# Layer 0 mixing on one core: product tiles with channels outermost, and the second gate spread over two passes

## The chip, the cores and the metric

The kernel runs on one core of a Trainium2 chip. The metric is the device time of one execution in microseconds, as the median of several runs.

## The reference, cut to what matters

The program is a chain of four image layers over x of shape (8, 56, 56, 192) in float32. Only layer 0 is touched. For every image it projects the normalised input three times (p, q and v, each with 576 channels and a silu), multiplies q by v, and convolves the product along the rows and along the columns with a decaying Toeplitz kernel of its own per channel. Then the sum of both is gated by p and projected back:

```python
qv = q * v
o1 = _toeplitz(qv.reshape(b * h, w, D1), a1).reshape(b, h, w, D1)
o2 = _toeplitz(jnp.transpose(qv, (0, 2, 1, 3)).reshape(b * w, h, D1), a2)
o2 = jnp.transpose(o2.reshape(b, w, h, D1), (0, 2, 1, 3))
out = p * (o1 + o2)
return out @ o_w.T + o_b
```

The result is added to the image, whose statistics the next layer uses.

## The kernel before, in words

Layer 0 has two steps. Step one computes q times v for all images and writes the operands of the convolution to two tensors in device memory, `left` and `right`. Step two, `layer0_mix`, is where the change lies.

**Products.** For one channel, both convolutions together are one matrix product: 56 x 128 by 128 x 56, where half of the 128 rows hold the Toeplitz matrix and half hold qv. The 576 channels are nine blocks of 64. A block is loaded by two transfers of 1.8 MB, `lt` and `rt`, from SyncE's queue (`layer0_block`); there are two buffers of each. From a block, eight channels (or twice eight) at a time are copied into a packed left operand `lc` by GpSimd and a packed right operand `rc`, alternately by VectorE and ScalarE (`layer0_operand`, L460). Each has three buffers, so copies run three iterations ahead of the products. `layer0_products` (L468) multiplies them into one of two PSUM tiles `op`, and ScalarE copies the result into a tile `o` in SBUF (L664 and L667).

**Passes.** The 576 channels of an image are worked off in three passes (`PASSES`). Passes one and two each take four blocks, two channels at once (on partitions 0 to 55 and 64 to 119), in 16 iterations; pass three takes the last block, one channel at once, in 8 iterations. Every pass allocates a tile `o` of 120 partitions from a pool of two buffers, laid out row of the image first, channel last: `o[partition, h, channel]`. The copy turns each result into this order by a strided view of PSUM.

**Gates.** When a pass is complete, its gate runs in steps, one or two of them after the products of each iteration of the following pass. The generators `layer0_gate` (for passes one and two) and `layer0_gate_last` (for pass three) yield between steps. For each of four tiles of 392 positions (times two halves), `layer0_gate` projects x to p for two groups of 128 channels (L478, PSUM tile `pj`), applies the silu on ScalarE into `pp` (L485), transposes the matching part of `o` on TensorE by seven transposes a half (L490, PSUM tile `ot`), multiplies `pp` by it on VectorE (L495), and multiplies by the output weights in three parts (L501, PSUM tile `y`), which VectorE adds to the image x (L507 and L509). The projection of the next tile is put ahead, between the transposes of the present one. `pj`, `ot` and `pp` have one buffer each. `layer0_gate_last` does the same for 64 channels, two tiles at a time, with narrower transposes (L552) in 8 steps in all.

A transpose loads its part of `o` as the stationary operand (128 channels of one image row for each partition) and streams an identity matrix through it.

**Order.** In `layer0_mix` the program order is written out by hand for TensorE, ScalarE, VectorE and GpSimd: each engine executes in the order in which the code issues. An iteration is: the products, the copy of the result into `o`, the copies for the operand three iterations ahead (the last operand of a block also issues the transfers of the block after next), then gate steps, then a step of side work. Side work is the normalised image `xn` for the gates (`normed`, L597, ScalarE, from iteration 10 of pass one; one buffer) and the statistics of the finished image (L607). The number of gate steps per iteration is, before the change:

```python
for _ in range((at // 8 % 2, 1, 2)[p]):
    next(gate, None)
```

So the last gate of the previous image takes a step in every other iteration of pass one, gate one takes one step in every iteration of pass two, and gate two takes two steps in every iteration of pass three. What is left of a gate is run at the end of its pass. After the last image the block buffers are closed (`loaded`), which lets the transfers for layer 1 into their place start; then the last gate of the last image runs alone, with the store and the statistics.

Of the kernel before, what the change touches and what calls it, by code (L numbers as in the profile page):

```python
# [24 lines left out]
NSUB = D1 // 64  # L25
# [66 lines left out]
def kernel(ctx: ExitStack, tc: tile.TileContext, a: dict, out: bass.AP):  # L92
# [377 lines left out]
    def layer0_gate(g, o, x, xn, pool, psum, w_p, w_o):  # L470
# [16 lines left out]
        def turn(t, s, pp):  # L487
            ot = psum.tile([128, 8, 128], F32, name="ot", bufs=1)
            for i in range(7):
                nc.tensor.transpose(  # L490
                    ot[:, i, 0:64 + W], o[:, H // 2 * s + 7 * t + i], ident[0:64 + W, 0:64 + W]
                )
# [19 lines left out]
        pp = new()  # L512
        silu(0, project(0, 0), pp)
        yield
        for t in range(NTH):
            silu(1, project(t, 1), pp)
            turn(t, 0, pp)
            yield
            if t + 1 < NTH:
                ps = project(t + 1, 0)  # L520
            turn(t, 1, pp)
            yield
            out(t, 0, pp)
            out(t, 1, pp)
            yield
            out(t, 2, pp)
            if t + 1 < NTH:
                pp = new()
                silu(0, ps, pp)
            yield  # L530

    def layer0_gate_last(o, x, xn, pool, psum, w_p, w_o):
# [4 lines left out]
        for t in range(0, NTH, 2):  # L537
# [12 lines left out]
            for s in range(2):  # L550
                for i in range(7):
                    nc.tensor.transpose(  # L552
                        ot[:, s, i * W:(i + 1) * W], o[0:W, 14 * s + 7 * (t // 2) + i, :], ident[0:W, 0:W]
                    )
# [25 lines left out]
    def layer0_mix(pool, raws, psum, ops, w_p, w_o, loaded):  # L580
# [44 lines left out]
        def right_operand():  # L625
            i = len(rcs)
            if i < len(todo):
                b, s, d0, nu = todo[i]
                rcs.append(layer0_operand(copies[i % 2], blocks[b * NSUB + s][1], "rc", 3, d0, nu, pool))

        def left_operand():
            i = len(lcs)
            if i < len(todo):
                b, s, d0, nu = todo[i]
                k = b * NSUB + s
                lcs.append(layer0_operand(nc.gpsimd.tensor_copy, blocks[k][0], "lc", 3, d0, nu, pool))
                if i + 1 < len(todo) and todo[i + 1][1] != s:
                    block(k + 2)
# [3 lines left out]
        for _ in range(3):  # L642
            right_operand()
            left_operand()
        n, gate, side, xn, before = 0, iter(()), iter(()), None, None
        for b in range(nimg):
            for p, (chunks, subs) in enumerate(PASSES):
                nu = len(chunks)
                o = pool.tile([64 + W, H, 128], F32, name="o")
                if p == 0 and b:  # L650
                    gate = layer0_gate_last(before, x[b - 1], xn, pool, psum, w_p, w_o)
                elif p:
                    gate = layer0_gate(p - 1, before, x[b], xn, pool, psum, w_p, w_o)
# [6 lines left out]
                for at in range(0, 64 // nu * len(subs), 8):  # L660
                    layer0_products(ops[n % 2], nu, lcs[n], rcs[n])
                    part = 64 * (nu - 1) + W
                    if p < 2:
                        nc.scalar.copy(o[0:part, :, at:at + 8], ops[n % 2][0:part].rearrange("p d h -> p h d"))  # L664
                    else:
                        two = o[0:part, 0:H // 2].rearrange("p (q i) (u d) -> p q u i d", i=7, u=2)
                        nc.scalar.copy(  # L667
                            two[:, :, :, :, at:at + 8],
                            ops[n % 2][0:part].rearrange("p d (q u i) -> p q u i d", u=2, i=7),
# [1091 lines left out]
```

## Time and profile before

| what | value |
|---|---|
| median of 3 runs | 5717.95 us (5717.43 to 5723.02) |
| profiled execution | 5735.38 us |
| its span | 5733.6 us |
| mean granted TensorE clock | 0.956 |
| TensorE busy | 5143.6 us, 90% of the span |
| products L468, 9216 matmuls | 354.7 us busy, first 788.9 us, last 2015.6 us |
| transposes L490, 896 | 119.9 us busy, 274 ns mean |
| transposes L552, 224 | 17.2 us busy, 225 ns mean |
| operand copies L460 by GpSimd, 320 | 587.2 us busy, 1853 ns mean |

Busy times of matmuls include the latency of each, and matmuls overlap; what one costs in a row of equals is read from the distance between starts. A float32 matmul of the program stands as two in the trace, a transpose as one. A line that begins with two numbers in the timeline gives start and length in microseconds, and in brackets how long the engine had been idle and which instruction ended that. A window's line gives its length, the busy time of each engine with its number of instructions, the granted clock, the share of the DMA engines' time and the rate in GB/s.

### The profile page before, as it was taken

Reading aid. Unit: us, or ns where it says so; the run is one execution under the profiler, and the core shown is the slowest. Engines: PE = TensorE matmul, PEld = TensorE weight load, DVE = VectorE, ACT = ScalarE, POOL = GpSimd, SP = SyncE. Lnnn points to the kernel's source line nnn. Section 1 sums busy time; section 2 is a strip of 40 time slices with the busy share of each in tenths; the row PEclk is TensorE's granted clock in tenths of the full one; section 3 lists DMA queues with packets and bytes.
Section 4 is the critical chain, followed back from the end, with each engine's and each line's share of the span. In section 5 each row is a group of like instructions: output and inputs, shape, how many; then the busy total and the mean of one; then the engine's idle time right before and its main releaser. Section 6 shows DMA issues by size and latency. Waiting matters only on the chain. (4 is left out here: it accounts for less than half of the span.)

```text
span 5733.6 us, 113240 instructions
## 1 busy us (share of the span) xinstructions
PE 5143.6 (90%) x49446; PEld 3417.5 (60%) x49446; DVE 3084.6 (54%) x4087; ACT 2285.5 (40%) x3100; POOL 1839.6 (32%) x1583
## 2 busy tenths in 40 slices
PE   7899968898999869999997989999798798999999
PEld 6798855565566535555554757776344597444444
DVE  4555534545445445666664868888778212433331
ACT  3344444444444423333332015454476300433333
POOL 5555554444444424333442013333011101101100
PEclk9999979999999989999998989999899898999999
DMA  6888895666666532222223856775677687212211
GB/s 155 226 228 225 219 307 224 246 251 240 249 234 254 209 94 70 78 74 74 78 66 91 266 229 216 232 242 188 173 226 209 228 328 289 73 62 77 79 39 26
DMA packets 556148, 1013.75 MB, mean 177 GB/s; under 512 B 256104, under 2 KB 479684, under 8 KB 528884
## 3 DMA queue, kind: packets, MB, share of 16 engines
q1 hardware_dynamic: 542896, 956.63, 52.2%
q0 software_dynamic: 8512, 40.62, 2.2%
q10 hardware_dynamic: 4244, 9.26, 0.6%
q8 instruction: 389, 6.37, 0.5%
q14 instruction: 107, 0.88, 0.0%
HBM read 676.92 MB, written 345.97 MB: 178 GB/s over the span
## 5 line engine op out<-in xcount | busy, mean ns | idle before, releaser
L460 POOL COPY lc<-lt 128x896 f32<-128x896 f32 (+1 forms) x320 | 587.2, 1853 | 640.9 <-PE op L468 600.3
L427 PE MATMUL qv<-w_qv_sb,x 64*112 64x256 f32 (+1 forms) x5376 | 686.9, 409 | 14.9 <-DVE act L433 11.0
L427 PEld LDWEIGHTS qv<-w_qv_sb,x 64*112 64x112 f32 x5376 | 605.9, 175 | 85.1 <-DVE act L433 21.1
L433 DVE TENSOR_TENSOR act<-qv,b_qv 112x640 f32<-112x640 f32 x448 | 318.5, 752 | 322.7 <-PE qv L427 233.2
L437 ACT ACTIVATE act<-act 112x640 f32<-112x640 f32 x448 | 300.5, 684 | 415.6 <-DVE act L433 405.1
L403 POOL TENSOR_TENSOR qv<-act 112x320 f32<-112x320 f32 x448 | 346.3, 797 | 291.2 <-ACT act L437 212.5
L468 PE MATMUL op<-rc,lc 128*56 128x56 f32 x9216 | 354.7, 224 | 77.4 <-POOL lc L460 29.9
L468 PEld LDWEIGHTS op<-rc,lc 128*56 128x56 f32 x9216 | 330.4, 139 | 152.8 <-issue 75.7
L1354 PE MATMUL ph<-y,w_sb 64*128 64x392 f32 x2304 | 398.3, 498 | 6.5 <-ACT hid L1358 6.5
L1365 PE MATMUL po<-hid,w_sb 128*64 128x392 f32 x2304 | 386.3, 494 | 0.0
L460 DVE COPY rc<-rt 128x896 f32<-128x896 f32 (+1 forms) x160 | 268.4, 1682 | 201.0 <-DMA rt<-right 107.4
L1372 DVE TENSOR_TENSOR x<-x,z 128x392 f32<-128x392 f32 x96 | 71.0, 740 | 522.0 <-ACT z L1370 522.0
L1081 PE MATMUL cv<-zc,wt 128*128 128x224 f32 x1536 | 313.3, 356 | 25.2 <-DMA zc<-pd 23.7
L1081 PEld LDWEIGHTS cv<-zc,wt 128*128 128x128 f32 x1536 | 290.4, 189 | 69.4 <-issue 54.4
L870 PE MATMUL qk_ps<-xr,wg 64*96 64x392 f32 x1536 | 329.4, 531 | 1.7 <-DVE xr L817 1.7
L478 PE MATMUL pj<-xn,w_p_sb 64*128 64x392 f32 x1536 | 292.3, 513 | 40.7 <-ACT pp L485 20.0
L1354 PEld LDWEIGHTS ph<-y,w_sb 64*128 64x128 f32 x2304 | 220.4, 189 | 176.4 <-issue 26.1
L915 POOL TENSOR_TENSOR e<-e,mx 128x1176 f32<-128x1176 f32 x64 | 140.0, 2187 | 561.6 <-DVE mx L914 536.5
L1255 PE MATMUL cps<-zc,wt 128*128 128x224 f32 x1536 | 299.4, 356 | 18.1 <-DMA zc<-zd 17.1
L501 PE MATMUL y<-pp,w_o_sb 128*64 128x392 f32 x1536 | 304.3, 505 | 12.6 <-DVE pp L495 12.6
L1096 POOL TENSOR_TENSOR rows<-rows,loc 128x896 f32<-128x896 f32 x96 | 223.5, 2328 | 270.3 <-ACT rows L1092 205.3
L1255 PEld LDWEIGHTS cps<-zc,wt 128*128 128x128 f32 x1536 | 289.4, 189 | 28.1 <-issue 20.6
(245 smaller groups left out, 8901.9 us busy)
## 6 DMA issues: line engine op xcount, KB each, us to landing
lt<-left SPq DMA_DIRECT2D x72, 1792.0 KB
rt<-right SPq DMA_DIRECT2D x72, 1792.0 KB
left<-qv SPq DMA_DIRECT2D x224, 252.0 KB
right<-qv SPq DMA_DIRECT2D x96, 504.0 KB
wt<-in_band_dram SPq DMA_DIRECT2D x23, 2048.0 KB
wt<-in_band_dram SPq DMA_DIRECT2D x11, 4096.0 KB
zc<-pd SPq DMA_DIRECT2D x187, 232.0 KB
pd<-pt SPq DMA_DIRECT2D x7, 5568.0 KB
```

What stands on the lines that cost most here:

```text
L403: nc.gpsimd.tensor_tensor(qv[:, s, s0:s1, k], *(acts[s][:, which, 0:n].rearrange("p (s d) -> p s d", d=64) for which in range(2)), ALU.mult,)
L427: nc.tensor.matmul(ps[s][:, which, 0:n], x[64 * s:64 * s + 64, j, bass.ts(i, 2 * W)], w_qv[64 * s:64 * s + 64, j, which, 64 * s0:64 * s1], ...
L433: nc.vector.tensor_tensor(acts[s][:, :, 0:n], ps[s][:, :, 0:n], b_qv[:, :, 64 * s0:64 * s1], ALU.add)
L437: nc.scalar.activation(acts[s][:, :, 0:n], acts[s][:, :, 0:n], AF.Silu)
L460: copy(c[:, 0:nu], raw.rearrange("p (w u d) -> p u d w", u=nu, d=64 // nu)[:, :, d0:d0 + 8])
L468: nc.tensor.matmul(op[64 * u:64 * u + W, i, :], lc[:, u, i], rc[:, u, i], start=True, stop=True)
L501: nc.tensor.matmul(y[64 * s:64 * s + 64], w_o[:, 2 * g + u, 64 * j:64 * j + 64], pp[:, u, s], start=(u == 0), stop=(u == 1),)
L870: nc.tensor.matmul(in_pairs(ps[s]), wg[64 * s:64 * s + 64, j, c0:c0 + HC], in_slots(xr[64 * s:64 * s + 64], (3 * g + j) * GW), start=(j == ...
L1081: nc.tensor.matmul(dst, wt[:, c4 + i, 128 * q:128 * q + 128], zc[:, :, c4 + i, q:q + NPAIR], start=(q == 0), stop=(q == 1),)
L1255: nc.tensor.matmul(dst.rearrange("p (b n) -> p b n", n=NPAIR), wt[:, c4 + i, q * OP:(q + 1) * OP], zc[:, :, c4 + i, q:q + NPAIR], start=(q ...
L1354: nc.tensor.matmul(ps[:, s, 0:TT], w0[64 * s:64 * s + 64, j, m * 128:(m + 1) * 128], y[64 * s:64 * s + 64, j, ts], start=(j == 0), stop=(j ...
L1365: nc.tensor.matmul(ps[64 * s:64 * s + 64], w1[:, m, 64 * j:64 * j + 64], hid[:, m, s], start=(m == 0), stop=(m == 5),)
```

## The change

Five things change in step two, and nothing elsewhere.

The tile `o` is laid out with channels outermost, `o[partition, channel, h]`, so that ScalarE's copy has the same order in source and destination, and a transpose takes 128 floats that lie 56 apart. There are two tiles with fixed roles in place of a pool of two: `os[0]` for pass one, `os[1]` for pass two. Pass three writes into channels 64 to 127 of `os[0]`, seen as a tile of 128 by 28 (`last`), which the last gate then reads. Gate two takes one step an iteration in pass three, where two of its four tiles fit, and nine further iterations of the next image's pass one do the rest; tile 2 begins with a projection of its own (`fresh`) in place of one put ahead. The last gate takes two steps in each of the first four iterations of pass one. Left and right operands have two buffers in place of three, so copies run two iterations ahead. After the last image, the last gate and then the rest of gate two run alone.

```diff
-    def layer0_gate(g, o, x, xn, pool, psum, w_p, w_o):
+    def layer0_gate(g, o, x, xn, pool, psum, w_p, w_o, fresh):
...
-                    ot[:, i, 0:64 + W], o[:, H // 2 * s + 7 * t + i], ident[0:64 + W, 0:64 + W]
+                    ot[:, i, 0:64 + W], o[:, :, H // 2 * s + 7 * t + i], ident[0:64 + W, 0:64 + W]
...
-        pp = new()
-        silu(0, project(0, 0), pp)
-        yield
         for t in range(NTH):
+            if t in fresh:
+                pp = new()
+                silu(0, project(t, 0), pp)
+                yield
             silu(1, project(t, 1), pp)
             turn(t, 0, pp)
             yield
-            if t + 1 < NTH:
+            ahead = t + 1 < NTH and t + 1 not in fresh
+            if ahead:
                 ps = project(t + 1, 0)
...
-                        ot[:, s, i * W:(i + 1) * W], o[0:W, 14 * s + 7 * (t // 2) + i, :], ident[0:W, 0:W]
+                        ot[:, s, i * W:(i + 1) * W], o[:, :, 14 * s + 7 * (t // 2) + i], ident[0:W, 0:W]
...
-                rcs.append(layer0_operand(copies[i % 2], blocks[b * NSUB + s][1], "rc", 3, d0, nu, pool))
+                rcs.append(layer0_operand(copies[i % 2], blocks[b * NSUB + s][1], "rc", 2, d0, nu, pool))
...
-                lcs.append(layer0_operand(nc.gpsimd.tensor_copy, blocks[k][0], "lc", 3, d0, nu, pool))
+                lcs.append(layer0_operand(nc.gpsimd.tensor_copy, blocks[k][0], "lc", 2, d0, nu, pool))
...
-        for _ in range(3):
+        for _ in range(2):
             right_operand()
             left_operand()
...
+        os = [pool.tile([64 + W, 128, H], F32, name=f"o{k}", bufs=1) for k in range(2)]
+        last = os[0][0:W, 64:128].rearrange("p d h -> p (d h)").rearrange("p (c r) -> p c r", c=128)
...
-                o = pool.tile([64 + W, H, 128], F32, name="o")
                 if p == 0 and b:
-                    gate = layer0_gate_last(before, x[b - 1], xn, pool, psum, w_p, w_o)
+                    first = layer0_gate_last(last, x[b - 1], xn, pool, psum, w_p, w_o)
                 elif p:
-                    gate = layer0_gate(p - 1, before, x[b], xn, pool, psum, w_p, w_o)
+                    gate = layer0_gate(
+                        p - 1, os[p - 1], x[b], xn, pool, psum, w_p, w_o, (0,) if p == 1 else (0, 2)
+                    )
                     next(gate)
...
-                        nc.scalar.copy(o[0:part, :, at:at + 8], ops[n % 2][0:part].rearrange("p d h -> p h d"))
+                        nc.scalar.copy(os[p][0:part, at:at + 8], ops[n % 2][0:part])
                     else:
-                        two = o[0:part, 0:H // 2].rearrange("p (q i) (u d) -> p q u i d", i=7, u=2)
                         nc.scalar.copy(
-                            two[:, :, :, :, at:at + 8],
-                            ops[n % 2][0:part].rearrange("p d (q u i) -> p q u i d", u=2, i=7),
+                            last.rearrange("p (u d) (q i) -> p d q u i", u=2, i=7)[:, at:at + 8],
+                            ops[n % 2][0:part].rearrange("p d (q u i) -> p d q u i", u=2, i=7),
                         )
...
-                    if p == 0 and at == 80:
+                    if p == 0 and i == 11:
                         xn = pool.tile([128, 3, NH], F32, name="xn0", bufs=1)
                         side = normed(b, x[b], xn)
-                    for _ in range((at // 8 % 2, 1, 2)[p]):
+                    if p == 0 and i < 4:
+                        next(first, None), next(first, None)
+                    elif p or i in (4, 5, 6, 7, 8, 9, 11, 12, 14):
                         next(gate, None)
                     next(side, None)
                 run(side)
-                run(gate)
-                before = o
+                if p < 2:
+                    run(gate)
         loaded()
-        run(layer0_gate_last(before, x[-1], xn, pool, psum, w_p, w_o))
+        run(layer0_gate_last(last, x[-1], xn, pool, psum, w_p, w_o))
+        run(gate)
```

More of the change, by code (lines that the diff above doesn't have):

```diff
@@ L526, in layer0_gate @@
             out(t, 2, pp)
-            if t + 1 < NTH:
+            if ahead:
                 pp = new()
@@ L641, in layer0_mix @@
         x = [load(0)]
-        for _ in range(3):
+        for _ in range(2):
             right_operand()
             left_operand()
-        n, gate, side, xn, before = 0, iter(()), iter(()), None, None
+        n, gate, first, side, xn = 0, iter(()), iter(()), iter(()), None
+        os = [pool.tile([64 + W, 128, H], F32, name=f"o{k}", bufs=1) for k in range(2)]
+        last = os[0][0:W, 64:128].rearrange("p d h -> p (d h)").rearrange("p (c r) -> p c r", c=128)
         for b in range(nimg):
@@ L659, in layer0_mix @@
                     x.append(load(b + 1))
-                for at in range(0, 64 // nu * len(subs), 8):
+                for i, at in enumerate(range(0, 64 // nu * len(subs), 8)):
                     layer0_products(ops[n % 2], nu, lcs[n], rcs[n])
```

## The prediction

> **What bounds the kernel now.** I read the page's slices first, then windows of the stage that the diff touches (about 780 to 2035 us), then the order of its matmuls and the waits in it. One image of that stage is three passes. The first copy of product tiles in each pass starts at 1405.08, 1449.19, 1508.40 and 1557.72 us in the timeline of ScalarE (image 4), so passes 1, 2 and 3 take 44.1, 59.2 and 49.3 us. Read the same way, the first pass takes 39.3 to 44.1 us in images 1 to 7, mean 42.6. The windows of these three passes (columns: PE, PEld, DVE, ACT, POOL busy, clock, DMA share, GB/s):
>
> ```profile
> 1405.00:1449.00 44.00, 32.87 (x647) 22.17 (x643) 25.11 (x18) 29.30 (x31) 31.72 (x16) 0.88 0.85 341
> 1449.00:1508.00 59.00, 56.83 (x747) 38.20 (x744) 34.87 (x41) 28.93 (x32) 29.39 (x16) 1.00 0.84 309
> 1508.00:1558.00 50.00, 46.70 (x411) 29.33 (x410) 17.49 (x24) 15.21 (x21) 12.88 (x9) 1.00 0.24 97
> ```
>
> The first pass moves 341 GB/s and leaves TensorE idle; the third is TensorE alone, with the DMA at 97 GB/s. One gate tile of the third pass, matmuls in order of time:
>
> ```profile
> 1521.12 2.25 PE L478 MATMUL pj<-xn,w_p_sb 64*128 64x392 f32 x12 [0.54 <-ACT pp L485]
> 1523.30 0.94 PE L490 MATMUL ot<-ident,o 120*128 120x120 f32 x7
> 1524.38 2.25 PE L478 MATMUL pj<-xn,w_p_sb 64*128 64x392 f32 x12
> 1526.56 0.94 PE L490 MATMUL ot<-ident,o 120*128 120x120 f32 x7
> 1527.43 1.03 PE L468 MATMUL op<-rc,lc 128*56 128x56 f32 x16
> 1528.29 4.43 PE L501 MATMUL y<-pp,w_o_sb 128*64 128x392 f32 x24
> 1532.25 0.99 PE L468 MATMUL op<-rc,lc 128*56 128x56 f32 x16
> ```
>
> By starts, a gate tile takes 2.18 + 1.08 + 2.18 + 0.87 + 3.96 = 10.27 us of TensorE, the third pass's products 0.87 an iteration. Four tiles less the first projection, which the second pass ends with, and eight iterations: 41.1 - 2.2 + 7.0 = 45.9, and some 2.8 of waits: the pass's 49.3. It is TensorE-bound. In the first pass, between matmuls:
>
> ```profile
> 1412.32 1.04 PE L468 MATMUL op<-rc,lc 128*56 128x56 f32 x32 [0.55 <-ACT o L664]
> 1418.43 1.58 PE L565 MATMUL y<-pp,w_o_sb 64*64 64x392 f32 x8 [5.08 <-DVE pp L555]
> ```
>
> and in VectorE's timeline:
>
> ```profile
> 1409.91 7.58 DVE L460 COPY rc<-rt 128x896 f32<-128x896 f32 x1 [2.06 <-PE op L468]
> ```
>
> The copy of a right operand hangs on a block whose transfer was issued at 1407.69; the gate's multiply is queued behind it on VectorE, and TensorE waits for that.
>
> **What the Trainium skill says.** SBUF — State Buffer, Specifications: lines are 16 bytes, and full bandwidth needs at least two hits a line. The trace agrees for ScalarE and GpSimd. L460 reads elements 128 or 256 bytes apart; L664 writes runs of 32 bytes from PSUM (min/median/max ns):
>
> ```profile
> L460 ACT COPY rc<-rt x160: 959/1799/2326, 787.0 to 1997.3; 128x896 f32<-128x896 f32 x128, 128x448 f32<-128x448 f32 x32
> L664 ACT COPY o<-op x256: 504/532/562, 795.9 to 1965.9; 120x448 f32<-120x448 f32 x128
> L490 PEld LDWEIGHTS ot<-ident,o x896: 137/140/144, 845.0 to 2014.5; 120*128 120x128 f32 x180
> L552 PEld LDWEIGHTS ot<-ident,o x224: 134/138/141, 954.2 to 2030.2; 56*128 56x128 f32 x112
> ```
>
> 448 more elements cost ScalarE 840 ns there, 1.875 ns each; the whole 448-element copy of L664 takes 532. TensorE: Matmul & The Clock Gate, LDWEIGHTS: the load is priced by columns (128 at P/1.2: 107 ns), and no stride is spoken of; the trace is faster, fourteen transposes of 56 columns in 1.07 us, 65 ns apart. The same page, Step-by-step: weights load ahead while a matmul runs. The trace agrees: seven wide transposes stand 112 ns apart ((0.94 - 0.27)/6), less than a load's 140 alone. ScalarE: Activation LUTs, What ACT_TABLE_LOAD costs: 186 + 0.833 N ns without pointers, 559 for N = 448; 532 measured.
>
> **The change, part by part.** *Layout.* The copies L664 and L667 become (nearly) contiguous. They are at full rate already, so I take nothing (between -0.1 us of each of 320, hidden mostly behind TensorE, and nothing). But the transposes' stationary operand, a slice of o, was 128 adjacent floats and becomes 128 floats 224 bytes apart. No row of this kernel shows a strided weight load. Lower bound: no cost, 112 and 65 ns stay. Upper: each weight costs what a strided element costs ScalarE, 128 x 1.875 = 240 ns, and the load, no longer covered by the previous matmul, sets the spacing: +128 ns for 896 wide transposes, +175 for 224 narrow ones, 115 + 39 = 154 us of TensorE. I take the upper value as the likeliest: [...]ScalarE and GpSimd (933 and 1802 ns for 448 and 896, 1.94 each) both pay; VectorE pays less (0.56 and 0.95 us, 0.87 each).
>
> *Gate two spread.* The third pass keeps two tiles: 20.5 - 2.2 + 7.0 + 1 = 26.3 us, 23.0 less. The first pass of the next image gets two tiles, 20.5. Its own TensorE work is 16 x 0.93 = 14.9 for products, 13.2 for the last gate (two times 2.13 + 1.0 + 1.4 + 1.3 + 0.8) and 2.2 for gate one's first projection: 30.3. With 20.5 that is 50.8; the three iterations without a gate step are held by GpSimd's 1.8 us copy, 2.7 more; the 2.5 us that ScalarE's normalisation (L597) holds the products stays: 56.0 against 42.6, +13.4. Blocks do not bind there any more: a block is used up in four iterations, about 14 us, and lands within 10 of its issue (1407.69 to the copy's end at 1417.5). No DMA is added or moved to another queue; only SyncE's block loads come one iteration later, with their need.
>
> *Buffers 3 to 2.* A copy for iteration n+2 starts after products n. Two iterations take 6 us in the second pass and a copy 1.8: no cost by itself. But right operands alternate between VectorE and ScalarE, and by one fewer ahead the parity turns: the program order puts ScalarE's copy into the iteration of the third output product, ahead of the next silu. Now that silu starts when the product ends, 1.3 us after the products; behind an eviction (0.1 + 0.53) and a copy (1.8) it starts at 2.4. The next projection, already 0.54 late in the lines above, waits for it because pj has one buffer: +1.05 x 3 tiles = 3.2 us a second pass. VectorE's copies move onto the iterations of the first two outputs, where it has room.
>
> *The shared tile and the end.* The third pass writes into the half of the first tile that gate one has finished with; the next first pass overwrites it from iteration 8, after the last gate's reads. The waits named in the program order are the same kinds as before. At the end, what layer 1 waits for is a transfer:
>
> ```profile
> 2048.85 0.72 POOL L767 MEMSET xr<- 128x720 f32 x1 [46.33 <-DMA x<-x]
> ```
>
> It starts when the last operand copy (1996.6) frees the blocks. That copy comes about 6 us sooner after the change; two gate tiles now run alone after the last gate: 1971.6 + 26 + 14.5 + 25, then 6 of statistics, 2043. About -4 us without dearer transposes, and +6 with them.
>
> **The sum**, without dearer transposes: third passes 7 x -23.0 = -161, first passes 7 x 13.4 = +94, second passes 8 x 3.2 = +26, the end -4: -45. Dearer transposes: a second pass 56 x 0.128 = 7.2, of which 95% shows (6.8); a third pass 28 x 0.128 = 3.6; a first pass 3.6 + 28 x 0.175 = 8.5, of which three quarters (6.4), as copies and normalisation leave room. Images 1 to 6: 16.8 each, 101; image 0 10.4; image 7 13.2 before its end; the end +10: 134. Together +89. The profiled execution took 5735.4 us around its span of 5733.6, so it would take 5824; the median of the runs shown is 17 lower, 5718, and gives 5807.
>
> **Rivals.** *Strided weights are nearly free* (the other side). Place: L490 and L552; price: the spacing. At no cost the time is 5718 - 45 = 5673; at double the narrow spacing (130 ns: +18 and +65, 31 us, 27 shown) it is 5700. It decides below 150 ns a transpose: (45/0.87 - 10.5)/1120 = 37 ns over 112. For it: VectorE's 0.87 ns, which gives 111 ns[...]; against: the other two engines' 1.9. *The first pass has no room*: VectorE's copies, stuck behind late blocks, hold the gate's multiplies, as at 1409.91, and with two buffers TensorE stops sooner. Then the tiles add to the 42.6 whole: 63.1, 7.1 more in seven passes, 50, with dear transposes 5857. For it: the 5.08 us wait shown; against: 14 us a block. *The change does not spread*: were the first pass held at its end by gate steps that the normalisation must wait for (one xn buffer), the gain would vanish and the dear transposes stay, 5718 + 134 = 5852; but the last projection stands at iteration 9 and the normalisation at 11.
>
> **How the numbers follow.** Dear transposes at 200 to 240 ns: 0.57, 5785 to 5835 (its own range). Double: 0.20, 5680 to 5720. Free: 0.15, 5655 to 5690. No room: 0.06. Not spread: 0.02. A range of 5680 to 5850 leaves out most of the free case and the worst of the last two, some 0.19. This kernel's measurement tells about 0.2% (11 us) from no change. Faster: 0.14 of free and 0.13 of double, 0.27; same 0.06; slower 0.67.
>
> **What would show it.** Right: the wide transposes near 240 ns apart, in seven of about 1.7 us, narrow ones in fourteen of about 3.3; a third pass of 30 us, a first of 62, a second of 69; DMA below 300 GB/s in the first pass. Wrong: L490 in seven of about 1 us; first passes over 65 with VectorE's copies waiting for blocks; or silu waiting no longer in second passes than before.

## The result and the profile after

The changed kernel takes 5648.5 us (median of 4 runs, 5640.4 to 5650.1); the kernel before took 5717.7 beside it (4 runs, 5715.9 to 5723.0). The ratio is 0.9875, with a 95% interval of 0.9857 to 0.9892: 1.25% faster. The forecast was 5807 and slower.

The span of the profiled execution is 5646.6 us, against 5733.6 before: 87.0 less. The medians differ by 69.2 only, because the profiled execution of the kernel before took 17 us more than its median, and that of the changed kernel took its median; where the 17 us lie is not known. The 87.0 are placed by reading the first copy of product tiles of every pass in ScalarE's timeline, as the prediction did:

| us | before | after |
|---|---|---|
| first pass, image 0 | 46.9 | 45.9 |
| first pass, images 1 to 7 | 39.3 to 44.1, mean 42.6 | 53.1 to 53.3 |
| second pass, images 0 to 6 | 57.5 to 62.5 | 60.4 to 60.6 |
| second pass, image 7 | 67.5 | 64.0 |
| third pass, images 0 to 6 | 49.3 | 26.2 |
| start of the last third pass to the start of layer 1 | 77.3 | 83.9 |

In sum: third passes 7 x -23.14 = -162.0; first passes +73.6 in images 1 to 7 and -1.1 in image 0; second passes +2.4; the end +6.7; the start of the stage -3.5. That is -84 of the -87.

The windows of image 4's three passes after the change (columns: window, length, then PE, PEld, DVE, ACT and POOL busy with their instructions, clock, DMA share, GB/s):

```profile
1350.50:1403.50 53.00, 50.13 (x753) 33.70 (x745) 25.25 (x29) 33.90 (x36) 33.23 (x17) 1.00 0.74 282
1403.50:1464.00 60.50, 57.09 (x732) 39.59 (x728) 34.79 (x40) 28.05 (x33) 26.92 (x17) 1.00 0.83 322
1464.00:1490.00 26.00, 25.46 (x295) 17.64 (x295) 10.31 (x14) 10.94 (x15) 13.03 (x8) 1.00 0.36 142
```

The first pass, which left TensorE idle for 11 of 44 us, now leaves it idle for 2.9 of 53, and moves 282 GB/s in place of 341. All three passes are bound by TensorE.

The granted clock is part of this. In image 4's first pass before the change, TensorE was granted half its clock in three stretches of 3.4 us, each of which begins in or just behind one of its three longest idle times there (5.08, 2.51 and 2.70 us). The windows of the three, and a projection that takes 2.25 us elsewhere:

```profile
1417.80:1421.20 3.40, 2.77 (x16) 0.80 (x16) 1.93 (x4) 0.00 (x0) 0.00 (x0) 0.50 0.97 409
1434.90:1438.30 3.40, 3.40 (x45) 2.09 (x44) 0.00 (x0) 3.40 (x4) 3.40 (x3) 0.50 0.98 417
1445.10:1448.50 3.40, 3.40 (x24) 1.68 (x22) 0.89 (x2) 0.58 (x1) 0.00 (x0) 0.50 0.90 346
...
1444.32 3.56 PE L478 MATMUL pj<-xn,w_p_sb 64*128 64x392 f32 x12 [2.70 <-DVE x L575]
```

In the first passes of images 1 to 7 such stretches add up to 10.2 us a pass, in 8.9 of which TensorE was busy: by estimate, at half speed, some 4.5 us a pass lost, or 31 in seven. After the change these passes have the full clock. No run changes the clock alone, but in all kernels here whose first passes leave TensorE idle for 2.7 to 4.0 us it is 1.00, and in those with 8.7 to 10.1 us it is 0.84 to 0.96.

What the forecast hung on is in the operations' own lines (min/median/max in ns), the wide and the narrow transposes and the copy of the product tile:

```profile
L490 PEld LDWEIGHTS ot<-ident,o x896: 185/198/208, 840.4 to 1945.1; 120*128 120x128 f32 x180
L554 PEld LDWEIGHTS ot<-ident,o x224: 189/213/217, 926.8 to 1918.9; 56*128 56x128 f32 x112
L669 ACT COPY o<-op x256: 508/532/577, 792.3 to 1876.5; 120x448 f32<-120x448 f32 x128
```

A load of 128 strided weights is 58 (wide) and 75 ns (narrow) longer than before, and the copy is what it was. What a transpose costs in a row shows in the order of the matmuls:

```profile
1412.78 2.25 PE L478 MATMUL pj<-xn,w_p_sb 64*128 64x392 f32 x12 [1.06 <-ACT pp L485]
1414.96 1.04 PE L490 MATMUL ot<-ident,o 120*128 120x120 f32 x7
...
1464.27 1.04 PE L490 MATMUL ot<-ident,o 120*128 120x120 f32 x7
...
1486.11 1.86 PE L554 MATMUL ot<-ident,o 56*128 56x56 f32 x14
```

Seven wide transposes take 1.04 us where they took 0.94; fourteen narrow ones 1.86 where they took 1.07. By their starts the wide ones stand 111 ns apart (102 before; the prediction's 112 came from durations, whose ends are modelled), the narrow ones 118 (62 before). Over the stage that is 896 x 9 + 224 x 56 = 20.6 us of TensorE. The first line shows the wait for the silu that the prediction named: 1.06 us, three times in each second pass.

The end of the stage, in the timelines of SyncE and of GpSimd:

```profile
1951.37 1.25 SPq L592 DMA_DIRECT2D x<-x  x2
...
1964.85 0.72 POOL L774 MEMSET xr<- 128x720 f32 x1 [59.50 <-DMA x<-x]
```

Layer 1 starts 13.5 us behind the issue of the last image's store. Before it was the same 13.5 (2035.38 to 2048.85).

### The profile page after: what moved, and what is told of

It is laid out like the page before. It is cut to its first block, busy times and chain, and to the rows that moved or that the text cites. A ratio compares the mean times of both kernels' runs of the same rounds, so it can differ in the third digit from the quotient of the medians.

```text
span 5646.6 us, 113339 instructions
## 1 busy us (share of the span) xinstructions
PE 5131.2 (91%) x49446; PEld 3421.6 (61%) x49446; DVE 3030.6 (54%) x4087; ACT 2287.3 (41%) x3100; POOL 1839.5 (33%) x1583
## 5 line engine op out<-in xcount | busy, mean ns | idle before, releaser
L1088 PEld LDWEIGHTS cv<-zc,wt 128*128 128x128 f32 x1536 | 290.1, 189 | 68.8 <-issue 53.2
L478 PE MATMUL pj<-xn,w_p_sb 64*128 64x392 f32 x1536 | 288.8, 508 | 32.7 <-ACT pp L485 31.6
L1262 PEld LDWEIGHTS cps<-zc,wt 128*128 128x128 f32 x1536 | 289.6, 189 | 28.1 <-issue 20.5
L460 DVE COPY rc<-rt 128x896 f32<-128x896 f32 (+1 forms) x160 | 215.3, 1346 | 150.4 <-PE op L468 96.8
```

The source lines that it names most:

```text
L460: copy(c[:, 0:nu], raw.rearrange("p (w u d) -> p u d w", u=nu, d=64 // nu)[:, :, d0:d0 + 8])
L1088: nc.tensor.matmul(dst, wt[:, c4 + i, 128 * q:128 * q + 128], zc[:, :, c4 + i, q:q + NPAIR], start=(q == 0), stop=(q == 1),)
L1262: nc.tensor.matmul(dst.rearrange("p (b n) -> p b n", n=NPAIR), wt[:, c4 + i, q * OP:(q + 1) * OP], zc[:, :, c4 + i, q:q + NPAIR], start=(q ...
```

## The experiments

### Layout alone

The kernel before with the channels outermost in `o`, in the copies and in the transposes, and nothing else.

```diff
-                    ot[:, i, 0:64 + W], o[:, H // 2 * s + 7 * t + i], ident[0:64 + W, 0:64 + W]
+                    ot[:, i, 0:64 + W], o[:, :, H // 2 * s + 7 * t + i], ident[0:64 + W, 0:64 + W]
...
-                o = pool.tile([64 + W, H, 128], F32, name="o")
+                o = pool.tile([64 + W, 128, H], F32, name="o")
...
-                        nc.scalar.copy(o[0:part, :, at:at + 8], ops[n % 2][0:part].rearrange("p d h -> p h d"))
+                        nc.scalar.copy(o[0:part, at:at + 8], ops[n % 2][0:part])
```

> The kernel before with channels outermost alone (three operand buffers, gates where they were; pass three uses half of its own tile). Theory A, strided weights are cheap: the trace of the changed kernel puts wide transposes 111 ns apart and narrow ones 118, where before it was 102 and 62 in a row. 896 x 9 + 224 x 56 ns = 20 us of TensorE, of which up to 18 show: 5718 to 5738 us, likeliest 5732. Theory B, that of the prediction, strided weights cost 240 ns and the spread of gate two hides it: 5718 + 125 = 5843. Theory C, the contiguous copies of ScalarE gain: below 5710.

Measured: 5733.5 against 5720.4, ratio 1.0023 (1.0012 to 1.0035): 13 us, with a third pass of 49.8 in place of 49.3. The strided weights cost what their spacing says, less what is hidden in the first pass (42.2 us in images 1 to 7, where the kernel before takes 42.6), and not 134 us.

### The rest of the change without the layout

The changed kernel with the image row first again in `o`, so that each transpose loads 128 adjacent floats. Pass three has a tile of its own, `last`, which holds the two halves of the image on partitions 0 to 55 and 64 to 119, so that two short copies an iteration take the place of one.

```diff
-        os = [pool.tile([64 + W, 128, H], F32, name=f"o{k}", bufs=1) for k in range(2)]
-        last = os[0][0:W, 64:128].rearrange("p d h -> p (d h)").rearrange("p (c r) -> p c r", c=128)
+        os = [pool.tile([64 + W, H, 128], F32, name=f"o{k}", bufs=1) for k in range(2)]
+        last = pool.tile([64 + W, H // 4, 128], F32, name="last", bufs=1)
...
+                        for s in range(2):
+                            half = last[64 * s:64 * s + W].rearrange("p (q i) (u d) -> p q u i d", i=7, u=2)
+                            nc.scalar.copy(
+                                half[:, :, :, :, at:at + 8],
+                                ops[n % 2][0:part, :, H // 2 * s:H // 2 * (s + 1)].rearrange(
+                                    "p d (q u i) -> p q u i d", u=2, i=7
```

> The changed kernel with image rows outermost again in both tiles, so that all weights are contiguous; pass three has a small tile of its own, its two halves on partitions 0 to 55 and 64 to 119, and two copies per iteration. Theory A: the strided weights cost the changed kernel 15 to 20 us, so 5630. Theory B: about 5520. If the layout plays no part: 5648.

Measured: 5625.4 us, ratio 0.9836 (0.9818 to 0.9853): 95 us below the kernel before and 23 below the changed one. First passes take 50.8 us, second 59.9, third 26.3. The spread gate, with two buffers, is the whole gain, and the layout gives about a quarter of it back. Some 3 of the 23 us, by estimate, are not the layout's: in the tile `last` fourteen narrow transposes take 0.88 us, less than the 1.07 of the kernel before, and there are sixteen such rows. This kernel beats both.

### Which strides are dear

Behind the last statistics of layer 0 in the changed kernel stand rows of fourteen matmuls on the same data, which differ only in the step between the 128 weights (the layer's own work is all there).

```diff
+        flat = os[0].rearrange("p d h -> p (d h)")
+        each = lambda step: flat[0:W, 0:127 * step + 1:step]
...
+        for i in range(14):
+            nc.tensor.transpose(at(i), each(1), eye)
+        for i in range(14):
+            nc.tensor.transpose(at(i), each(2), eye)
...
+            nc.tensor.transpose(at(i), each(56), eye)
```

> The changed kernel with rows of fourteen matmuls added after the statistics of the last image, where TensorE waits: transposes of 56 columns whose stationary operand takes 128 floats 1, 2, 3, 4, 8, 16 and 56 apart, then ordinary float32 matmuls with such weights (1, 4, 56), then with such a moving operand of 128 columns (1, 4, 56). Theory A, a weight load pays for each new 16-byte line, up to a limit reached at 4 floats: 62 ns apart at 1, between at 2 and 3, and 118 from 4 on, all the same. Theory A2, the cost grows with the distance: 56 dearer than 4. Ordinary float32 weights [...]should not be slower at 4 or 56; nor should a moving operand, if the same limit of some 0.9 ns an element holds. Rival: a moving operand pays double, as ScalarE's reads do.

The weight loads, by line (step 1 at L700, 2 at L702, 4 at L706, 56 at L712), with the first and last start of fourteen:

```profile
L700 PEld LDWEIGHTS ot<-ident,o x14: 135/138/141, 1952.6 to 1953.4; 56*128 56x128 f32 x14
L702 PEld LDWEIGHTS ot<-ident,o x14: 192/213/216, 1953.5 to 1955.0; 56*128 56x128 f32 x14
L706 PEld LDWEIGHTS ot<-ident,o x14: 212/217/218, 1956.7 to 1958.3; 56*128 56x128 f32 x14
L712 PEld LDWEIGHTS ot<-ident,o x14: 199/200/201, 1961.5 to 1962.9; 56*128 56x128 f32 x14
```

With step 1 the starts are 62 ns apart, with any other step 110 to 120: the price is one of adjacent or not, and the distance does not count. It is whole at step 2 already, which neither theory had. The granted clock fell in the row of step 8, so that steps 16 and 56 and the ordinary matmuls behind them ran at half of it (windows of steps 1 to 4, of steps 16 and 56, and of ordinary matmuls):

```profile
1952.50:1958.30 5.80, 5.80 (x56) 5.71 (x56) 5.60 (x12) 0.00 (x0) 0.00 (x0) 1.00 0.77 175
1959.90:1962.90 3.00, 3.00 (x30) 3.00 (x29) 1.33 (x3) 0.00 (x0) 0.00 (x0) 0.50 0.97 245
1962.90:1981.90 19.00, 19.00 (x88) 19.00 (x86) 3.49 (x7) 1.90 (x4) 2.70 (x4) 0.50 0.31 94
```

For step 56 at the full clock the changed kernel has 118 ns, beside 120 for steps 2 and 4 here, so the reading holds. The Trainium skill, SBUF — State Buffer, Specifications, says that 16-byte lines need two hits each for full bandwidth and that each crossing to a new line costs; with step 2 a line of four floats has its two hits, and the row takes 120 ns all the same, as with step 4, so for these loads the measurement differs from the page. In ordinary float32 matmuls of the same run (two instructions each in the trace), at half the clock, strided weights cost some 20 ns an instruction, 233 in place of 213; a strided moving operand of 128 columns costs 14 to 25 ns (227 and 238), and not double. At the full clock these were not measured.

### Whose turn it is to copy

In the changed kernel VectorE and ScalarE change places in the right operands, so that ScalarE's copy no longer stands ahead of the next silu in the second pass.

```diff
-        copies = (nc.vector.tensor_copy, nc.scalar.copy)
+        copies = (nc.scalar.copy, nc.vector.tensor_copy)
```

> The changed kernel with the two engines of the right operand copies exchanged, so that VectorE copies in the iterations of the first transposes' second half and of the third output product, as it did before the change, and ScalarE in the others. Theory A: the silu of the next tile starts 1.05 us sooner three times a second pass, and once in the third: 8 x 3.3 = 26 us, 5622. Rival: VectorE's copy then delays the multiplies and additions by as much, and nothing is won: 5640 to 5655.

Measured: 5647.1 us, ratio 0.9876 (0.9859 to 0.9894), which is the changed kernel's own time. Second passes fall from 60.5 to 59.4, but first passes rise from 53.1 to 53.7 and the last second pass from 64.0 to 65.3. TensorE's waits for the silu fall from 31.6 to 18.1 us over the stage, and the time does not: taking the silu's wait away is not a gain by itself.

### Two and three buffers

The kernel before with two buffers of each operand, and the changed kernel with three.

```diff
-                rcs.append(layer0_operand(copies[i % 2], blocks[b * NSUB + s][1], "rc", 3, d0, nu, pool))
+                rcs.append(layer0_operand(copies[i % 2], blocks[b * NSUB + s][1], "rc", 2, d0, nu, pool))
...
-                lcs.append(layer0_operand(nc.gpsimd.tensor_copy, blocks[k][0], "lc", 3, d0, nu, pool))
+                lcs.append(layer0_operand(nc.gpsimd.tensor_copy, blocks[k][0], "lc", 2, d0, nu, pool))
...
-        for _ in range(3):
+        for _ in range(2):
```

> The kernel before with two left and two right operand buffers in place of three, nothing else. Theory A, only the parity counts: 3 x 1.05 in second passes and 3 x 0.3 in third passes, 8 x 4 = 33 us, less what waits for blocks already hide: 5735 to 5750. Rival, the lookahead itself counts, as first passes are held by late blocks and stop sooner: first passes above 46 us, 5760 to 5780. Rival, neither: 5718.

Measured: 5712.1, ratio 0.9987 (0.9976 to 0.9998), 8 us less in place of 33 more. Second passes are 59.8 to 60.1 in images 0 to 6, where the kernel before scatters from 57.5 to 62.5, and 3.0 us shorter in the sum of all eight. TensorE's waits for the silu rise as foreseen, from 20.0 to 38.4 us over the stage, and the waits of the gate's multiply behind a late right operand (12.6 us) go. Third passes do not change, and most of what the stage wins is in the first passes, 10.8 us in sum (a mean of 41.2 in place of 42.6 in images 1 to 7).

> The changed kernel with three left and three right operand buffers, as before the change. This also turns the parity of the right operand copies back. Theory A, the first pass is bound by TensorE and not by copies or blocks: first passes 53 us as now, second passes 59 to 60.5, so 5640 to 5650. Rival, the lookahead is missed in the first pass: first passes 50 us, 5625.

Measured: 5655.5, ratio 0.9879 (0.9859 to 0.9899), which the ratio does not tell from the changed kernel's 0.9875: the third buffer would win nothing there. TensorE's waits for the silu fall from 31.6 to 18.7 us over the stage, but 15.1 us of waits for the gate's multiply are there again, 12.0 of them behind a late right operand, and some second passes take 63.4 to 63.6 us, since VectorE's copy meets late blocks in their seventh iteration. Why it meets them with three buffers and not with two was not tried. First passes take 53.8 us, near the 53 of the first theory.

### The end

The contiguous kernel, with gate two of the last image not spread (two steps an iteration in its third pass, where no first pass follows), and then with the turns of the right operands exchanged as well.

```diff
-                        p - 1, os[p - 1], x[b], xn, pool, psum, w_p, w_o, (0,) if p == 1 else (0, 2)
+                        p - 1, os[p - 1], x[b], xn, pool, psum, w_p, w_o, (0,) if p == 1 or b + 1 == nimg else (0, 2)
...
                         next(gate, None)
+                        if p == 2 and b + 1 == nimg:
+                            next(gate, None)
```

> The spread kernel with contiguous weights, and gate two of the last image alone at its old pace of two steps an iteration, so that after the last image only the last gate runs alone. Theory A, the start of layer 1 waits for the store of the last image, which follows the last gate step: that store stands 70 us after the start of the last third pass in the changed kernel and 64 in the kernel before, so 6 us less than the same kernel without it: 5619. Rival, a load bounds the start of layer 1, as the prediction said: 5625, or later as the block buffers come free later.

Measured: 5626.8, ratio 0.9828 (0.9809 to 0.9847), the same as without this edit. From the start of the last third pass the store is issued after 63.5 in place of 66.4 us, but layer 1 starts after 78.9 in place of 79.8. In both it starts when the second half of the store has landed, and this now comes 15.4 us behind the store's issue in place of 13.5. The loads of layer 1's first image, which SyncE issues ahead of the store as soon as the block buffers come free, go out from 33.8 in place of 19.4 us, and their last packets end at 68.3 in place of 53.5. All runs are alike in this: where the loads go out from 33.8 us or later, layer 1 starts 15.1 to 15.8 us behind the store's issue; where they go out by 26.3, 13.3 to 13.5. So the first theory has the wait right, and the second is right that the loads set how soon it can end; the loads were not moved by themselves.

> As the one before, and the engines of the right operand copies exchanged. Theory A, the silu wait goes (3 x 0.85 us a second pass) but a wait for a block in iteration 14 gives 1.5 back: 5 to 10 us less than without, 5612. Rival, it is all given back: 5619.

Measured: 5654.9, ratio 0.9873 (0.9853 to 0.9894): 28 us above the kernel without the exchange, which neither theory had. Second passes are 1.1 us shorter; first passes take 52.9 to 57.7 in place of 50.8. Four of images 1 to 7 take 54.3 to 57.7 and the others 52.9 to 53.2, and each of the four, and no other, holds a VectorE copy of 3.7 to 5.4 us. The changed kernel with the same exchange has none; why was not tried. One, in the timeline of image 5's first pass (columns: start, length, engine and line):

```profile
1524.11 5.33 POOL L460 COPY lc<-lt 128x896 f32<-128x896 f32 x3 [2.71 <-PE op L468]
1524.86 5.37 DVE L460 COPY rc<-rt 128x896 f32<-128x896 f32 x1 [0.75 <-PE op L468]
1530.15 0.96 DVE L495 TENSOR_TENSOR pp<-pp,ot 128x784 f32<-128x784 f32 x1
1531.16 4.21 PE L501 MATMUL y<-pp,w_o_sb 128*64 128x392 f32 x13 [3.02 <-DVE pp L495]
```

GpSimd makes three left-operand copies without a gap; the copy on VectorE starts among them and ends 0.79 us behind the last. The gate's multiply is queued behind it, and TensorE waits 3 us. The same stands in the profile of the kernel before, around the copy of 7.58 us that the prediction showed:

```profile
1405.17 11.54 POOL L460 COPY lc<-lt 128x896 f32<-128x896 f32 x6 [2.61 <-PE op L468]
...
1417.57 0.51 SPq L452 DMA_DIRECT2D rt<-right  x1
...
1419.85 0.94 DVE L460 COPY rc<-rt 128x896 f32<-128x896 f32 x1 [1.47 <-DMA rt<-right]
```

That copy ended at 1417.49, 0.78 us behind six copies of GpSimd (1416.71). It did not wait for the transfer issued at 1407.69: that one was waited for by the next copy, at 1419.85, and the buffer that the long copy read was refilled as soon as it ended (1417.57). All seven VectorE copies of over 3 us before the change, one in each first pass of images 1 to 7, lie within such runs; after the change there is none. The 112 of VectorE's copies of 896 elements that overlap a GpSimd copy before the change have a median of 2.02 us, the 16 others of 0.93. The Trainium skill, SBUF — State Buffer, Who interferes with whom, names a cause: VectorE and GpSimd share a pair of ports, a copy between SBUF tiles can take it, and the one that is second is blocked for the whole instruction of the first. The trace agrees in kind, but the copy of 7.58 us was held through four GpSimd copies, and not through one. That led to the next two runs.

### VectorE beside GpSimd

The changed kernel with a measurement behind the last statistics of layer 0: copies of 896 strided floats alone, and beside four copies of GpSimd in a row. `left_run(n)` is a short memset on GpSimd, which releases the other engine, and n copies.

```diff
+        left_run(0)
+        nc.vector.tensor_copy(to, far)
+        left_run(4)
+        nc.vector.tensor_copy(to, far)
+        left_run(0)
+        nc.scalar.copy(to, far)
+        left_run(4)
+        nc.scalar.copy(to, far)
...
+        for i in range(4):
+            nc.vector.tensor_copy(to, far)
+        nc.gpsimd.tensor_copy(free[:, 0:16 * W].rearrange("p (u d w) -> p u d w", u=2, d=8), far)
```

> The changed kernel with a measurement added behind the last statistics of layer 0: each kind of copy of 896 floats into a right operand once with nothing on GpSimd, and once started while GpSimd makes four left-operand copies one after the other. Theory A (VectorE and GpSimd share a way into SBUF, and the one that comes second waits until the other pauses): VectorE's strided copy takes about 0.95 us alone and over 6 us beside the four (until about 0.8 us behind their end); ScalarE's stays at 1.8; VectorE's product of a PSUM and an SBUF operand stays at about 0.97. Theory B (the long copies of the kernel before hung on a late block, as the prediction read them): VectorE's copy takes under 1.5 us in both cases. Four VectorE copies in a row, with a GpSimd copy started behind the first: A: GpSimd's takes about 1.8 plus what is left of the four, some 5 us; B: under 2.6.

The timelines (L706: GpSimd's four copies; VectorE's copy alone at L711, beside them at L713; ScalarE's at L715 and L717; VectorE's product of a PSUM and an SBUF operand at L723 and L725; four copies of VectorE at L728):

```profile
1964.30 0.85 DVE L711 COPY rc<-o 120x896 f32<-120x896 f32 x1
1965.29 7.33 POOL L706 COPY o<-o 120x896 f32<-120x896 f32 x4
1965.34 2.45 DVE L713 COPY rc<-o 120x896 f32<-120x896 f32 x1 [0.20 <-POOL rc L704]
...
1972.69 1.70 ACT L715 COPY rc<-o 120x896 f32<-120x896 f32 x1 [22.44 <-POOL rc L704]
1974.59 2.08 ACT L717 COPY rc<-o 120x896 f32<-120x896 f32 x1 [0.19 <-POOL rc L704]
...
1989.32 0.97 DVE L723 TENSOR_TENSOR rc<-ot,o 120x784 f32<-120x784 f32 x1 [4.88 <-POOL rc L704]
1990.49 0.97 DVE L725 TENSOR_TENSOR rc<-ot,o 120x784 f32<-120x784 f32 x1 [0.20 <-POOL rc L704]
...
1996.12 7.47 DVE L728 COPY rc<-o 120x896 f32<-120x896 f32 x3
```

VectorE's copy goes from 0.85 to 2.45 us beside GpSimd: it ends 0.8 us behind the first of GpSimd's copies, of 1.73, and the next of them takes 2.40. The product with a PSUM operand takes 0.97 both times, as the page says of instructions with one SBUF operand. So the interference is real and belongs to VectorE's copies. But here one copy was waited out, not four: the "over 6 us" of the first theory was missed. In the last row it is more than one again. The fourth VectorE copy, beside GpSimd's:

```profile
1999.34 4.25 DVE L728 COPY rc<-o 120x896 f32<-120x896 f32 x1
...
1998.47 2.44 POOL L729 COPY o<-o 120x896 f32<-120x896 f32 x1
2000.84 0.73 POOL L810 MEMSET xr<- 128x720 f32 x1
2001.50 0.11 POOL L811 MEMSET xr<- 128x15 f32 x1
2001.55 1.38 POOL L1527 MEMSET e<- 128x1536 f32 x1
```

It starts within the copy and ends 0.66 us behind the third memset. Why VectorE is let in after one GpSimd instruction in some places, and passed over by four in others, stays open. GpSimd's copy in this row takes 2.44 us and not the 5 of the first theory. ScalarE's copy takes 1.70 alone and 2.08 beside GpSimd, which no theory had; it is one sample.

### GpSimd with one copy less ahead

The kernel before with two left operands (GpSimd's) and three right ones, so that the turns of the right operands stay and GpSimd runs no long series. The transfers of a block are issued by GpSimd's copies and so come one iteration later, too.

```diff
-                lcs.append(layer0_operand(nc.gpsimd.tensor_copy, blocks[k][0], "lc", 3, d0, nu, pool))
+                lcs.append(layer0_operand(nc.gpsimd.tensor_copy, blocks[k][0], "lc", 2, d0, nu, pool))
...
-        for _ in range(3):
+        for _ in range(2):
             right_operand()
             left_operand()
+        right_operand()
```

> The kernel before with two left operands (GpSimd's) and three right ones as before: the turn of VectorE and ScalarE stays, only GpSimd runs no longer up to six copies in a row. Theory A (GpSimd's runs of copies hold VectorE's copy in the first pass): the longest VectorE copy falls from 7.6 to under 4 us, TensorE's wait of 5 us for the last gate's multiply goes, first passes take about 39 in place of 42.6, and the time is 15 to 30 us below the kernel before, about 5698. Theory B (the copy hangs on a late block): the 7.6 us copies stay and the time is that of the kernel before, 5718 within 10.

Measured: 5740.0 against 5725.6, ratio 1.002 (1.0009 to 1.0031): 14 us slower. The mechanism held: no VectorE copy takes over 3.5 us. The gain did not come. In the list of TensorE's waits (total, times, longest), the kernel before had

```profile
PE y L565 <- DVE pp L555: 27.2, 7, 5.1
PE op L468 <- DVE rc L460: 23.7, 5, 13.9
PE op L468 <- POOL lc L460: 5.7, 3, 4.2
```

and this kernel has, with no wait of L565 for L555 left,

```profile
PE op L468 <- POOL lc L460: 37.7, 36, 3.2
PE op L468 <- DVE rc L460: 33.3, 9, 12.1
```

The 27 us of the multiply came back as 42 of waits for the operands themselves. First passes are 40.4 to 44.4 us in images 1 to 7, as before, with TensorE idle for 9.8 us in place of 10.1 and the granted clock at 0.85 to 0.92. Removing the longest wait of these passes moved TensorE's idle time and did not shorten it. In the profiled executions the loss is in the second passes, which are 8.7 us longer in sum; whether the later transfers make it was not tried.

### Gate steps ahead of the copies

The contiguous kernel with the end not spread, and the two operand copies of an iteration put behind its gate step in program order, so that silu and multiply stand ahead of them.

```diff
-                    right_operand()
-                    left_operand()
                     n += 1
...
                             next(gate, None)
+                    right_operand()
+                    left_operand()
                     next(side, None)
```

> The fastest so far (contiguous weights, last gate two not spread) with the two operand copies of an iteration put behind its gate step in program order, so that silu and the gate's multiply stand ahead of them on ScalarE and VectorE. Theory: the three waits of 1.05 us for the silu in each second pass go, and no held copy can hold a multiply: 8 x 2.5 to 3.2 = 20 to 25 us less than 5627, about 5604; second passes about 57.5, first passes 50 to 51. Rival: with the copies later and two buffers, products wait for operands: as fast as or slower than 5627.

Measured: 5623.1, ratio 0.9821 (0.9804 to 0.9839), against 0.9828 (0.9809 to 0.9847) without this edit: not told apart. The stage itself did what was forecast. In TensorE's waits the silu falls from 30.7 us to

```profile
PE pj L478 <- ACT pp L485: 10.4, 41, 0.8
```

and second passes take 57.2 us in place of 59.8, first passes 51.9 in place of 50.8. Layer 1 starts 11 us sooner. In the profiled executions layer 1's last projection of queries and keys starts no sooner (2977.9 against 2975.3 us); the granted clock in the windows of layer 1 was lower with this kernel, 0.95 in four windows of 100 us where the other had it in two. Whether the 11 us are lost by the lower clock or by chance was not settled.

## Why the prediction was wrong

The forecast lies 158 us above the result, on the other side of no change. The result lies even below the 5655 to 5690 that the prediction gave to free transposes, so more than one term was off.

**Dear transposes: wrong, and the failed step.** "I take the upper value as the likeliest": 240 ns for each weight load, 134 us in the sum. Measured: 111 ns for the wide, 118 for the narrow, 13 us for the layout alone and 23 between the two versions of the change. The step carried a rate of ScalarE's copies (1.875 ns an element) over to another engine's weight loads. The kernel's own profile had two rates for strided reads, and the prediction named both; VectorE's 0.87 ns gives the 111 ns that were found, which may be chance. Two engines had the dear rate and one the cheap one, but nothing in the profile tied the weight loads to either. (The copies behind these rates read elements 256 bytes apart in every pass, by the rearrangement in `layer0_operand`, and never 128.) The mechanism has a second half that was named too: the load was to set the spacing once it grew. It grew to 198 ns for the wide transposes, yet they stand 111 apart: the loads overlap one another. The rival's decision point (37 ns more a transpose) was the right question; 9 and 56 ns, a mean of 18, fall on its other side. This step alone made the sign.

**Third passes: right.** 26.3 forecast without dear transposes, 26.2 measured, with the strided weights in it.

**First passes: too long in work and in waits.** Without dear transposes 56.0 was forecast, 50.8 of work and 5.2 of waits for GpSimd's copies and the normalisation. With contiguous weights a first pass takes 50.8, but TensorE is busy for 47.6 of it and idle for 3.2, so that the forecast's work equals the measured pass by chance; with strided weights it is 50.2 and 2.9. The work was too long by a reading: the last gate's outputs were priced at 3.5 us (1.4 + 1.3 + 0.8) from lines of which most ran at half the clock, and take 2.1 in the changed kernel, twice a pass. The waits were too long as well. Together this is 36 us in seven passes. One more reading was wrong: the 7.58 us copy of VectorE did not hang on a block, but among GpSimd's copies. The rival "no room" rested on the same reading, and first passes of 63 did not come.

**Second passes: wait right, its balance wrong.** The silu waits 1.06 us three times a pass, as forecast, and in second passes TensorE's waits for it went from 5.8 to 26.3 us in sum, 20.5 more, where 26 was forecast (of the 20.0 before, 14.2 stood in third passes). But the five waits of 1.0 to 3.0 us for a multiply behind a late right operand, 12.6 in sum, went at the same time, and the granted clock, 0.95 to 0.97 in the second passes of images 1, 5 and 7, became 1.00 in all but the last (0.97). So all second passes together grew by 2.4 us. The step counted the new wait and not what goes with it. The kernel before with two buffers shows the same exchange: silu waits of 25.2 us in second passes, no multiply waiting behind a late operand, and second passes 3.0 us shorter in sum.

**The end: size right, cause wrong.** Forecast were -4 without dear transposes and +6 with them; +6.7 came, with cheap ones, which is luck. What layer 1 waits for is the store of the last image, which follows the last gates, and not a transfer that starts when the block buffers come free. Such transfers count in another way, as the run with the end not spread shows: issued later, they go with a later landing of the store.

Without dear transposes the prediction's sum was -45; the version with contiguous weights measured -95 between the medians and -105 between the profiled executions. Of the 60 us between -45 and -105, 37 are first passes and 29 second passes that came out shorter than forecast, less 6 at the end.

## What to carry to other kernels

Where the profile shows two rates for the same kind of access on different engines, and none for the engine in question, the forecast should stand between them until a row of fourteen instructions has measured it. Work that moves from a pass bound by one engine into a pass that leaves it idle fills idle time, and the waits there go rather than add up: 20.5 us of gate work made a first pass 8 to 10 us longer, with TensorE's idle time down from 10.1 to some 3 us and its clock up from 0.88 to 1.00. What a matmul costs should be read where the granted clock is the one that the changed kernel will have. A single long wait in a pass with several limits is not worth its length: taking away 27 us of it gave 42 us of others.

## What the runs showed of the hardware

A float32 transpose whose 128 weights are not adjacent costs 110 to 120 ns in a row, at step 2 (120) as at step 56 (118, and 110 at half the clock); with adjacent weights it costs 62 ns for 56 columns streamed and 102 for 120. So the stride shows in full where few columns are streamed, and hardly where 120 are.

ScalarE's copy of 448 elements from PSUM takes 532 ns whether it reads in order or with a step of 224 bytes, while its strided copy of 896 elements from SBUF takes 1.8 us.

A VectorE copy between SBUF tiles of 0.95 us took up to 7.6 us beside GpSimd's copies, and 2.45 and 4.25 in a measurement by itself; a VectorE product with a PSUM operand took 0.97 with GpSimd and without.

TensorE was granted half its clock for 10.2 us, on average, of first passes that left it idle for 10.1, and the full clock in first passes that left it idle for 2.7 to 4.0.
